# Half of the grouped attention's weights turned by VectorE blocks and DMA instead of TensorE, values two groups behind; the first sequence of the first attention turned by TensorE

## The chip, the cores and the metric

One core of a Trainium2 chip runs one kernel, from the inputs in DRAM to the output in DRAM. The metric is the device time in microseconds of that one launch. All data are fp32. PE is TensorE, DVE VectorE, ACT ScalarE, POOL GpSimd; SP issues the DMAs.

## What is computed

Eight sequences of 256 tokens with 512 features go through four layers in turn. Layers 0 to 2 begin with attention, and that is what the change touches. Layer 0: RMS norm with a conditioned scale, 8 query heads of 64 on one key and value head, rotary positions, softmax, values, output projection, residual; then a gated MLP. Layer 1: 16 heads of 32 with normed queries and keys, then a GELU MLP. Layer 2 has a grouped attention, and no MLP:

```
h = layernorm(x) * (1 + scale) + shift
q = rope(h @ Wq.T)                     # 16 heads of 32
c = h @ Wkd.T                          # 128 latent features
k, v = rope(c @ Wku.T), c @ Wvu.T      # 4 key and value heads of 32
s = q @ k.T / sqrt(32)                 # a key head for 4 query heads
s = where(mask, -inf, s)               # later blocks of 128 and all beyond a window of 64,
                                       # but for every 64th key, are hidden
x = x + (softmax(s) @ v) @ Wo.T
```

Layer 3 applies eight small experts to slices of the features, then a conditioned norm and a projection.

## The kernel before

The x of all sequences stays in SBUF as 16 tiles of 128 tokens. The layers follow each other: attention 0 (some 0 to 290 us of the profile), MLP 0 (to 905), attention 1 (to 1250), MLP 1 (to 1660), grouped attention (1672 to 1941), layer 3.

All three attentions are written by one function, `attend`. Its loop runs over 8 sequences and the groups of a sequence, four heads each: 2 groups in attention 0, 4 in the others. For a group it issues:

- the scores (`scored`, L692): for each head and block of 128 queries a matmul into one of four PSUM banks "A"; a bank is free again when the softmax of the head that was in it is done with it. In the grouped attention the first 128 queries see 128 keys and the others 256, so a head has 384 columns.
- the softmax (`softmax`): in the grouped attention DVE adds the mask and takes the row maximum in one custom instruction, with a second one that reads the accumulator into `low` (L730; in attention 0 it is a plain maximum, L714). ACT takes the exponential with the row sum (L734). A reciprocal of the sums (L745), a small DVE transpose (L749) and two DMAs over DRAM (L752, L757) spread the inverse sums.
- the turning of the weights, since the values product needs keys on partitions. There are two ways. By PE: 128x128 transposes against the identity (`turned`, L769) into a bank "C", and a copy back to SBUF (L478 on DVE for even places, L481 on ACT for odd ones). In blocks, for heads 0 and 1 of a group: the scores are taken with the keys in block order, the exponentials go to one tile for both heads, DVE turns its 32x32 blocks (L739), four DMAs put the tile to a DRAM tile `flip` (`put`, L546), and one gets it back (L743); the block of the right partitions then lies in place. `in_blocks` tells how many heads of a group go in blocks: two in attention 0 and 1 for sequences 0 to 6, none for sequence 7, none in the grouped attention.
- the values product one group behind (`weighted`, L794), and the multiplication with the inverse sums into the context (`divided`, L811).

Between these steps a queue of other work is fed in by portions (`some`, `quantum`): the projection of the next sequence (`project0`, `project2`: L628 from hT and wqkv; DVE's rope at L646 and L647; POOL's sums at L1650 and L1655; the copies at L1642 and L1654; the turned queries and keys at L1236 and L1242 with copies at L478 to L482) and the output projection of the last one (L628 from wo, addition to x at L1293). The portions come from costs written by hand in the call (`work`).

The input hT of a projection is prepared for a later sequence: norms (L448 to L468), DVE block transpose (L532), put to DRAM (L546), `fetch` back (eight DMAs, L564), and `modulate`, which scales it by DVE (L488) and ACT (L489) in turn. In attention 0 the norms are turned by PE (L498).

Attention 0 starts with the loads; DVE works out the angles of the rotary positions (`angles`: L1160 to L1192), ACT their sines (L1193 to L1196); PE works out conditions from weights that come from DRAM (L315, L333).

Within a program each engine takes its instructions in a fixed order, and SP its DMAs. That order comes from a scheduler of the framework, which starts from the order of the program's text; it isn't written out by hand. So a change in the text can move instructions that it does not name.

Of the kernel before, what the change touches and what calls it, by code (L numbers as in the profile page):

```python
# [34 lines left out]
P = 128  # L35
B, S, D = 8, 256, 512
NT = B * S // P
TB = S // P
# [59 lines left out]
def constants():  # L98

    f32 = np.float32  # L100
    freqs = (f32(1.0) / f32(10000.0) ** (np.arange(0, 32, 2, dtype=f32) / f32(32))).astype(f32)
    ang = np.arange(S, dtype=f32)[:, None] * freqs[None, :]
    cos = np.cos(ang.astype(np.float64)).astype(f32)
    sin = np.sin(ang.astype(np.float64)).astype(f32)
    rope = np.stack([np.concatenate([cos, cos], 1), np.concatenate([-sin, sin], 1)], 1)
    rope = rope.reshape(TB, P, 2, 32).transpose(1, 0, 2, 3)
    i, k = np.arange(S)[:, None], np.arange(S)[None, :]
    hidden = ((np.abs(k - i) > 64) & (k % 64 != 0)) | (k // P > i // P)
    mask = np.where(hidden, f32(MASKED), f32(0.0))
    mask = np.concatenate([mask[:P, :P], mask[P:, :]], 1)  # L110
    return {
        "inv_freq": np.array([INV_FREQ], f32),
        "rope2": np.ascontiguousarray(rope),
        "mask2": np.ascontiguousarray(mask),
    }


# [61 lines left out]
class Program:  # L179
# [357 lines left out]

    def in_blocks(self, name, b):

        return 2 if name != "attention2" and b < B - 1 else 0  # L540

    def put(self, kept, tile):

# [106 lines left out]


    def attend(self, name, n_groups, hd, project, value, finish, work, key_tiles=(2, 2), biased=None,
               extra=None, then=None, spare=None, inverse=None, after=None):

# [41 lines left out]
        def softmax(s, b):  # L698
            n_blocks = self.in_blocks(name, b)
            tot = self.t([P, 4, TB], "tot", 3)  # L700
            lows = self.t([P, 4, TB], "low", 3)

            blocks = self.t([P, 8 * P], "p")[:, : 2 * total]
            if n_blocks:
                put = blocks.rearrange("p (c h x) -> p h c x", c=4, h=2)
                ps = []
            else:
                ps = [blocks[:, j * total : (j + 1) * total] for j in range(2)]
            plain = self.t([P, 2, 512], "p")
            ps += [plain[:, j, :total] for j in range(2)]  # L710
            for j in range(4):
                low = lows[:, j, :]
                if biased is None:
                    nc.vector.tensor_reduce(  # L714
                        low, s[j].rearrange("p (q k) -> p q k", q=TB), AX.X, ALU.max, negate=True
                    )
                for q in range(TB):
                    cols = slice(at[q], at[q] + wide[q])
                    src, sign, out = s[j][:, cols], 1.0, None
                    if j >= n_blocks:  # L720
                        out = ps[j - n_blocks][:, cols]
                    else:
                        out = put[:, j, :, at[q] // 4 : (at[q] + wide[q]) // 4]
                        src = src.rearrange("p (c x) -> p c x", c=4)
                    if biased is not None:
                        by = biased[j < n_blocks][:, cols]
                        if j < n_blocks:
                            by = by.rearrange("p (c x) -> p c x", c=4)

                        nc.vector.tensor_tensor_reduce(  # L730
                            out, src, by, -1.0, BIG, ALU.add, ALU.min, low[:, q : q + 1]
                        )
                        src, sign = out, -1.0
                    nc.scalar.activation(  # L734
                        out, src, AF.Exp, bias=low[:, q : q + 1], scale=sign,
                        accum_out=tot[:, j, q : q + 1],
                    )
                if j == 3 and n_blocks:
                    nc.vector.transpose(blocks, blocks)  # L739
                    kept = self.flips[self.n_flip % 4][:, : 2 * total]  # L740
                    self.n_flip += 1
                    self.put(kept, blocks)
                    nc.sync.dma_start(blocks, kept)  # L743
            inv = self.inv[self.n_spread % 2]
            nc.vector.reciprocal(  # L745
                inv[:, 0 : 4 * TB].rearrange("p (j q) -> p j q", q=TB), tot
            )
            inv_t = self.t([P, 32], "invT", 2)
            nc.vector.transpose(inv_t, inv)  # L749

            kept = self.spread[self.n_spread % 4]
            nc.sync.dma_start(kept.rearrange("c (b r) -> b c r", b=4), inv_t)  # L752
            rows = kept.rearrange("(j q) t -> j (q t)", q=TB)
            by = []
            for c in range(nch):
                t = inverse[(self.n_spread * nch + c) % 4]
                nc.sync.dma_start(  # L757
                    t, rows[c * per : (c + 1) * per, :].unsqueeze(1).to_broadcast([per, hd, S])
                )
                by.append(t)  # L760
            self.n_spread += 1
            return (blocks, ps), by
# [43 lines left out]
        def divided(b, o, by):  # L806
            for c in range(nch):
                chunks = ctx.setdefault(b, [])
                out = spare()[len(chunks)] if b == late else self.t([P, S], "ctxT")
                in_ = o[:, c * S : (c + 1) * S]  # L810
                nc.vector.tensor_tensor(out, in_, by[c], ALU.mult)  # L811
                chunks.append(out)

        def outcome(b):
            chunks = ctx.pop(b)
            return finish(b, lambda k, t: chunks[k][:, t * P : (t + 1) * P])

        last, steps, done = None, [], []
        for i in range(B * n_groups + 1):
            ahead = None  # L820
            if i < B * n_groups:
# [18 lines left out]
                    turned(j + len(weights) % 4 // 2, p)  # L840
            if ahead is not None:
                ahead = (b, g, softmax(ahead[2], b))
                if g == 0 and ahead_of:
                    for c in (1, 2) if b == 0 else (b + 2,):
                        if c < B:
                            steps.append(self.prepare(name, c, quick=c == 1))
                        elif c == B and after is not None:
                            steps.append(self.prepare(after, 0))
                elif g == 0 and b == B - 1:
                    steps.append(self.prepare(after, 0))  # L850

                for step in steps:
                    for _ in step:
                        if b > 0 and ahead_of:
                            break
                    else:
                        done.append(step)
                steps[:] = [step for step in steps if step not in done]
# [17 lines left out]
                self.end = end  # L876
            else:
                self.some(quantum)
                b, g, (pT, by) = last
                weights = pT[1]  # L880
                for j, p in enumerate(weights[len(weights) // 2 :]):
                    turned(j + len(weights) % 4 // 2, p)
                self.some(quantum)
                divided(b, weighted(b, g, pT), by)
                if g == n_groups - 1:
                    if b != late:
                        self.queue.insert(0, outcome(b))
                    got.pop(b)
                self.some(quantum)
            if ahead is not None and ahead[1] == n_groups - 1:  # L890
                self.modulate()
# [726 lines left out]
    def load_layer2(self):  # L1618
        nc, d = self.nc, self.d
        w = self.t([P, KC, 1536], "wqkv", pool=self.wqkvp)  # L1620
        self.load(w[:, :, 0:512], "wq2T")
        self.load(w[:, :, 512:640], "wkdT")
        nc.sync.dma_start(w[:, 0, 640:896], d["wkvuT"])
        self.w2 = w
        self.w2o = self.t([P, KC, D], "wo", pool=self.wop)
        self.load(self.w2o, "wo2T")
        rope = self.bank("row")[:, 0 : TB * 64].rearrange("p (t c s e) -> p t c s e", t=TB, c=2, s=2)
        nc.sync.dma_start(rope.rearrange("p t c s e -> p t c (s e)"), d["rope2"])
        self.rope2 = rope
        self.mask = self.bank("row")[:, :384]  # L1630
        nc.sync.dma_start(self.mask, d["mask2"])

    def project2(self, b, got):
        nc, w = self.nc, self.w2
# [38 lines left out]
    def layer2(self):  # L1673
# [2 lines left out]
        self.attend(  # L1676
            "attention2", 4, 32, self.project2, lambda v, g, j, k: v[:, k, j * 32 : (j + 1) * 32],
            lambda b, ctxT: self.added(b, ctxT, self.w2o), (10.4, 6.8), key_tiles=(1, 2),
            biased=(self.mask,), extra={7: (self.expert_inputs(0), 1.74)},
            spare=lambda: [spare[:, i, :] for i in range(4)],  # L1680
            inverse=[spare[:, i, :] for i in range(4, 8)],
        )


# [178 lines left out]
```

## Time and profile before

| | |
|---|---|
| three runs, median | 2103.41 us (2102.42 to 2107.41) |
| the profiled execution | 2102.78 us |
| its span | 2100.7 us |
| mean granted clock of TensorE | 0.989 |
| DMA: moved, share of 16 engines | 182.48 MB, 29.3% |
| ACT exponentials L734, 128x256 (and others) | x512, 240.0 us |
| PE transposes of weights L769 | x816, 122.3 us |
| DVE mask and maximum L730 | x400, 127.8 us |

How to read the profile. Times are in microseconds from the span's start, unless marked ns; L12 is line 12 of the kernel before. A group row gives line, engine, operation, out<-in by tile names, shapes and count, then busy time and the mean of one in ns, then the idle time of the engine just before these instructions and what ended most of it. A timeline row gives start, duration, engine, line, operation; a bracket at its end gives the idle time ahead of it and its releaser. The duration of one PE or ACT instruction overlaps with its neighbours, so prices are better read from start to start. PEld is the weight load, which lies beside PE's matmuls. PEclk is the clock that TensorE was granted, in tenths of full speed in the page, as a fraction in tables by stretch. A row of waits gives who waited for whom: total, times, longest.

### The profile page before, as it was taken

What the parts mean: (1) busy time and instruction counts of PE and PEld (TensorE: products, weight loads), DVE (VectorE), ACT (ScalarE), POOL (GpSimd) and SP (SyncE); (2) the same over time, 40 slices, a digit from 0 to 9 for tenths busy, and PEclk for the clock granted to TensorE, in tenths of its full rate; (3) what the DMA queues carried; (4) which work ended last, traced back from release to release, by engine and by line L of the source; (5) the groups of instructions that cost most, each with busy time, mean ns of one, the idle gap of its engine ahead of it and who ended that gap; (6) DMA issues with size and microseconds to landing.
All of it is one profiled execution on the core that took longest, in us unless ns stands there. A gap on an engine that the chain in (4) does not pass through costs nothing.

```text
span 2100.7 us, 36220 instructions
## 1 busy us (share of the span) xinstructions
PE 2034.6 (97%) x12946; PEld 1486.9 (71%) x12946; DVE 1348.9 (64%) x4432; ACT 743.7 (35%) x2330; POOL 302.7 (14%) x340
## 2 busy tenths in 40 slices
PE   7799999999999999999999999999999999999999
PEld 4455569999999999854544448999999755555444
DVE  6677766666676555756676675767666777676233
ACT  4233421111111111146566652222222265556543
POOL 1111200000000000054445621000000111010220
PEclk8999999999999999999999999999999999999999
DMA  9543451212130010335455542235211321210001
GB/s 317 161 139 94 115 202 39 72 42 64 62 108 26 16 32 16 97 95 140 130 145 142 150 132 87 86 92 155 63 46 36 89 44 38 58 38 21 9 36 40
DMA packets 202659, 182.48 MB, mean 87 GB/s; under 512 B 81200, under 2 KB 169200, under 8 KB 202480
## 3 DMA queue, kind: packets, MB, share of 16 engines
q1 hardware_dynamic: 202480, 180.17, 29.3%
q8 instruction: 103, 1.69, 0.3%
q14 instruction: 76, 0.62, 0.1%
HBM read 122.16 MB, written 57.97 MB: 86 GB/s over the span
## 4 chain that ended last, share of the span: by engine, by line
PE 82%; DVE 6%; ACT 6%; DMA 3%; POOL 2%; issue 1%; SPq 0%; ACTq 0%; DVEq 0%; POOLq 0%
PE C L1002 28%; PE C L628 21%; PE A L1051 18%; ACT p L734 4%; PE A L692 4%; PE C L794 3%; PE C L769 3%; PE A L1731 1%; PE C L1750 1%; ACT p L481 1%; DVE st L448 1%; DVE p L730 1%; DMA hT<-turn 1%; PE C L315 1%; DVE n L647 1%
## 5 line engine op out<-in xcount | busy, mean ns | idle before, releaser
L1002 PE MATMUL C<-hT,wbig 128*128 128x128 f32 x3072 | 416.4, 275 | 1.0 <-DVE p L1025 1.0
L1002 PEld LDWEIGHTS C<-hT,wbig 128*128 128x128 f32 x3072 | 388.7, 192 | 10.1 <-issue 3.5
L628 PE MATMUL C<-wqkv,hT 128*128 128x512 f32 (+1 forms) x768 | 314.7, 551 | 0.4 <-ACT v L1490 0.4
L734 ACT ACTIVATE p<-p,low 128x256 f32<-128x256 f32 (+1 forms) x512 | 240.0, 471 | 165.8 <-DVE low L730 154.5
L1051 PE MATMUL A<-wbig,p 128*128 128x256 f32 x1024 | 242.2, 379 | 0.0
L628 PEld LDWEIGHTS C<-wqkv,hT 128*128 128x128 f32 x768 | 131.7, 193 | 122.7 <-issue 108.7
L1051 PEld LDWEIGHTS A<-wbig,p 128*128 128x128 f32 x1024 | 189.7, 190 | 23.1
L1032 DVE TENSOR_TENSOR p<-p,C 128x256 f32<-128x256 f32 x192 | 79.0, 419 | 164.3 <-PE C L1002 162.3
L1022 ACT COPY p<-C 128x128 f32<-128x128 f32 x192 | 50.8, 265 | 367.5 <-PE C L1002 359.0
L628 PE MATMUL C<-wo,ctxT 128*128 128x512 f32 x336 | 159.8, 609 | 2.9 <-DVE ctxT L811 2.9
L1002 PE MATMUL C<-ctxT,wbig 128*128 128x128 f32 x1152 | 160.0, 275 | 0.0
L1002 PE MATMUL C<-qk,wbig 128*128 128x128 f32 x1152 | 159.8, 275 | 0.0
L456 POOL TENSOR_SCALAR r<-mv 128x2 f32<-128x2 f32 (+1 forms) x28 | 7.0, 252 | 967.7 <-DVE mv L449 967.7
L730 DVE CUSTOM_DVE_ANT_0 p<-A,row 128x256 f32<-128x256 f32 (+1 forms) x400 | 127.8, 377 | 26.6 <-PE A L692 24.9
L1002 PEld LDWEIGHTS C<-ctxT,wbig 128*128 128x128 f32 x1152 | 144.1, 192 | 0.0
L1002 PEld LDWEIGHTS C<-qk,wbig 128*128 128x128 f32 x1152 | 144.0, 192 | 0.0
L769 PEld LDWEIGHTS C<-ident,p 128*128 128x128 f32 x816 | 92.2, 142 | 64.3 <-issue 37.8
L769 PE MATMUL C<-ident,p 128*128 128x128 f32 x816 | 122.3, 282 | 4.8 <-DVE p L478 1.9
L1374 ACT ACTIVATE p<-C 128x128 f32<-128x128 f32 x64 | 17.7, 277 | 302.4 <-DVE p L1032 302.4
L1023 DVE TENSOR_TENSOR p<-p,C 128x128 f32<-128x128 f32 x192 | 54.7, 285 | 96.6 <-ACT p L1022 95.6
L628 PEld LDWEIGHTS C<-wo,ctxT 128*128 128x128 f32 x336 | 59.5, 191 | 67.7 <-issue 55.2
L734 ACT ACTIVATION_READ_ACCUMULATOR p<-p,low 128x1 f32 x512 | 96.2, 188 | 0.0
(227 smaller groups left out, 3224.6 us busy)
## 6 DMA issues: line engine op xcount, KB each, us to landing
flip<-p SPq DMA_DIRECT2D x168, 128.0 KB
p<-flip SPq DMA_DIRECT2D x42, 512.0 KB
turn<-hT SPq DMA_DIRECT2D x120, 128.0 KB
hT<-turn SPq DMA_DIRECT2D x16, 512.0 KB
kept<-hT SPq DMA_DIRECT2D x16, 512.0 KB
hT<-kept SPq DMA_DIRECT2D x16, 512.0 KB
wbig<-spread SPq DMA_DIRECT2D x64, 128.0 KB
hT<-turn SPq DMA_DIRECT2D x112, 64.0 KB
```

Source lines behind the costliest of these rows:

```text
L315: self.nc.tensor.matmul(m[32 * i : 32 * i + 32, :], cond[:, k, :], w[c // 512][:, k, c % 512 : c % 512 + width], start=(k == 0), stop=(k = ...
L628: self.nc.tensor.matmul(out, lhsT(k), rhs(k), start=(k == 0), stop=(k == n - 1))
L692: nc.tensor.matmul(s[j][:, at[q] : at[q] + wide[q]], lhsT(q), keys, start=True, stop=True,)
L730: nc.vector.tensor_tensor_reduce(out, src, by, -1.0, BIG, ALU.add, ALU.min, low[:, q : q + 1])
L734: nc.scalar.activation(out, src, AF.Exp, bias=low[:, q : q + 1], scale=sign, accum_out=tot[:, j, q : q + 1],)
L769: nc.tensor.transpose(m[:, n * P : (n + 1) * P], p[:, at[q] + k * P : at[q] + (k + 1) * P], self.ident,)
L794: mm = nc.tensor.matmul(o[i * hd : (i + 1) * hd, c * S + q0 * P : (c + 1) * S], value(got[b][1], g, j, k), weights(j, mine), start=(k == 0 ...
L1002: nc.tensor.matmul(m[:, c : c + P], w[:, k * P : (k + 1) * P], b[:, k], start=(first and k == 0), stop=(k == steps - 1), skip_group_check= ...
L1022: nc.scalar.copy(g[:, 0, :], m[:, 0:P])
L1023: nc.vector.tensor_tensor(g[:, 0, :], g[:, 0, :], m[:, P : 2 * P], ALU.add)
L1032: nc.vector.tensor_tensor(g[:, 1:3, :], g[:, 0, :].unsqueeze(1).to_broadcast([P, 2, P]), m[:, 2 * P : 4 * P].rearrange("p (i t) -> p i t", ...
L1051: nc.tensor.matmul(acc[at][:, half * S : (half + 1) * S], left, right, start=(p == 0 and half == 0), stop=(p == 3), skip_group_check=True,)
```

## The change

In the grouped attention heads 0 and 1 of each group of sequences 0 to 6 are turned in blocks; sequence 7 stays with PE. The copies of the two heads that PE still turns both go to ACT. Each group's weights lie in one of four "rooms" (tiles of 128x2048), its contexts in halves of one tile for two sequences; the mask is held a second time in block order, loaded by one more DMA. The values product of these groups stands two groups behind (`lag`, `due`), not one. In attention 0 sequence 0 is turned by PE, not in blocks.

By count, before and after: L769 in the program 816 and 664; DVE copies of 128x384 in the grouped attention 56 fewer; DVE block transposes of 128x768 28 more, of 128x1024 two fewer; puts and gets of `flip` 140 more in the grouped attention and ten fewer in attention 0; in attention 0 four more DVE copies of 128x512. The order of the instructions differs on all engines in these two attentions, and is the same in the MLPs and in attention 1.

```diff
@@ in_blocks
-        return 2 if name != "attention2" and b < B - 1 else 0
+        first = {"attention0": 1, "attention1": 0, "attention2": 0}[name]
+        return 2 if first <= b < B - 1 else 0
@@ softmax
-            blocks = self.t([P, 8 * P], "p")[:, : 2 * total]
+            if rooms is None:
+                blocks, plain = self.t([P, 8 * P], "p"), self.t([P, 2, 512], "p")
+            else:
+                room = rooms[self.n_spread % 4]
+                blocks, plain = room[:, : 8 * P], room[:, 8 * P :]
+                plain = plain.rearrange("p (j x) -> p j x", j=2)
+            blocks = blocks[:, : 2 * total]
...
-            plain = self.t([P, 2, 512], "p")
@@ divided
-                out = spare()[len(chunks)] if b == late else self.t([P, S], "ctxT")
+                if b == late:
+                    out = spare()[len(chunks)]
+                elif contexts is not None:
+                    out = contexts[:, b % 2 * 4 + len(chunks), :]
+                else:
+                    out = self.t([P, S], "ctxT")
@@ the loop over groups
+                lag = 2 if rooms is not None and self.in_blocks(name, b) else 1
+                due.append((i + lag, *ahead))
...
-                divided(b, weighted(b, g, pT), by)
-                if g == n_groups - 1:
-                    if b != late:
-                        self.queue.insert(0, outcome(b))
-                    got.pop(b)
+                while due and due[0][0] <= i:
+                    _, b, g, (pT, by) = due.pop(0)
+                    divided(b, weighted(b, g, pT), by)
+                    if g == n_groups - 1:
+                        if b != late:
+                            self.queue.insert(0, outcome(b))
+                        got.pop(b)
@@ load_layer2
-        self.mask = self.bank("row")[:, :384]
+        self.mask = both[:, TB * 64 :]
         nc.sync.dma_start(self.mask, d["mask2"])
+        self.mask_blocks = self.bank("row")[:, :384]
+        nc.sync.dma_start(self.mask_blocks, d["mask2_blocks"])
@@ layer2
-            biased=(self.mask,), extra={7: (self.expert_inputs(0), 1.74)},
+            biased=(self.mask, self.mask_blocks), extra={7: (self.expert_inputs(0), 1.74)},
...
+            rooms=[self.t([P, 4 * 512], "wbig") for _ in range(4)],
+            contexts=self.t([P, 8, S], "wbig"),
```

## The prediction

> **What bounds the kernel now.** First the page: busy times, granted clock and the chain that ended last.
>
> ```profile
> PE 2034.6 (97%) x12946; PEld 1486.9 (71%) x12946; DVE 1348.9 (64%) x4432; ACT 743.7 (35%) x2330; POOL 302.7 (14%) x340
> ...
> PEclk8999999999999999999999999999999999999999
> ...
> PE 82%; DVE 6%; ACT 6%; DMA 3%; POOL 2%; issue 1%; SPq 0%; ACTq 0%; DVEq 0%; POOLq 0%
> ```
>
> TensorE is the bound: only 66 us of the 2100.7 us span are not PE work. An edit gains what it takes off PE and loses every PE idle that it opens. Next the groups of the grouped attention (1672 to 1941 us), shapes kept apart:
>
> ```profile
> L769 PE MATMUL C<-ident,p 128*128 128x128 f32 x372 | 54.7, 280 | 3.4 <-DVE p L478 1.9 <-ACT qT L482 1.5
> ...
> L478 DVE COPY p<-C 128x384 f32<-128x384 f32 x62 | 33.9, 546 | 0.4
> ```
>
> These are the weights' transposes and their copies by VectorE. The mean of 280 ns overlaps with its neighbours, so the price is read from PE's timeline, at the start of a sequence:
>
> ```profile
> 1848.33 0.94 PE L692 MATMUL A<-v,qT 32*128 32x128 f32 x16
> 1849.19 0.98 PE L769 MATMUL C<-ident,p 128*128 128x128 f32 x7
> 1850.02 1.89 PE L628 MATMUL C<-hT,wqkv 128*128 128x256 f32 x8
> 1851.74 1.88 PE L628 MATMUL C<-wqkv,hT 128*128 128x512 f32 x4
> 1853.56 1.37 PE L794 MATMUL C<-p,kT 128*32 128x256 f32 x16
> ```
>
> From start to start seven transposes take 0.83 us, 119 ns each, a group's scores (L692) 0.86 us. After the first scores of a sequence stands the projection of the next (L628 from hT), without any idle. The table by stretches says how full each engine is, and when the clock was halved (columns: length, PE, PEld, DVE, ACT, POOL busy, granted clock, DMA share, GB/s):
>
> ```profile
> 289.60:293.00 3.40, 1.62 (x3) 0.59 (x4) 1.00 (x5) 0.00 (x0) 0.00 (x0) 1.00 0.14 48
> 293.00:296.40 3.40, 3.40 (x5) 1.34 (x4) 2.43 (x6) 0.00 (x0) 0.00 (x0) 0.50 0.83 237
> ...
> 914.30:917.70 3.40, 2.21 (x13) 1.38 (x13) 3.40 (x14) 0.94 (x4) 0.00 (x0) 1.00 0.98 358
> 917.70:928.00 10.30, 10.30 (x32) 6.44 (x31) 8.07 (x34) 7.37 (x28) 0.00 (x0) 0.50 0.29 82
> ...
> 1740.30:1743.70 3.40, 2.09 (x22) 1.30 (x19) 3.09 (x13) 1.78 (x6) 1.68 (x2) 1.00 0.04 7
> 1849.00:1858.00 9.00, 9.00 (x66) 5.03 (x59) 5.50 (x25) 4.62 (x19) 0.00 (x0) 1.00 0.23 56
> 1815.00:1849.40 34.40, 32.85 (x232) 17.97 (x231) 24.72 (x112) 19.52 (x77) 3.38 (x4) 1.00 0.23 49
> ```
>
> One sequence of the grouped attention is the last row: PE 32.9 of 34.4 us, DVE 24.7, ACT 19.5. Last, PE's waits, and ACT's timeline in the longest:
>
> ```profile
> PE C L1242 <- ACT v L481: 10.3, 1, 10.3
> ...
> PE C L794 <- DMA p<-flip: 1.5, 1, 1.5
> ```
>
> ```profile
> 65.27 0.52 ACT L1193 ACTIVATE row<-row 128x384 f32<-128x384 f32 x1 [16.30 <-DVE row L1192]
> ...
> 67.17 0.24 ACT L481 COPY v<-C 128x128 f32<-128x128 f32 x1
> ```
>
> In the first attention PE stands for 10.3 us since a copy of v waits on ACT behind a sine that waits for DVE's angles.
>
> **Transposes and copies.** In 28 groups (seven sequences by four) 6 of 12 transposes go: 168 x 0.119 = 20.0 us off PE; by the tightest and loosest pace that I find in the trace (0.109 and 0.135) 18.3 to 22.7. The two copies per group go from DVE: 56 starts at 0.47 (L478 at 1851.51, the next at 1851.98), 26.3 us; one DVE transpose of 128x768 comes. The trace has that of 1024 columns in the second attention:
>
> ```profile
> L739 DVE STREAM_TRANSPOSE p<-p 128x1024 f32<-128x1024 f32 x28 | 34.8, 1244 | 5.8 <-ACT p L734 5.8
> ```
>
> Three quarters are 0.93 us, 28 times 26 us. DVE's sum stays the same, with 9.7 us free in a sequence. L730 in block form costs what the plain form costs (418 and 419 ns per 256 columns in the second attention): nothing. Here a rule speaks against the change: the Trainium skill, "VectorE: DVE Perf Modes", Rules for kernel authors, gives a full 128x128 transpose to TensorE. It looks at the operation alone (390 ns there, against 311 by DVE in 32x32 blocks, both for bf16). By it the six transposes stay where they are and the gain is zero; by the rows PE has 119 ns each and is the bound, DVE 155 (0.93 / 6) with time to spare, so the 20.0 us stand.
>
> **The DMAs.** Per group SP issues four puts and one get more, 140 in all, 0.8 MB moved in a group's 8.6 us, about 90 GB/s beside 49; the DMA share is 0.23. Two groups (17 us) lie between turn and use; in the second attention one group was enough but for a single wait of 1.5 us. So the weights arrive: nothing (0 to 2 us). But the puts wait on SP for DVE's transpose, and the fetch of the next hT now stands behind them, in order.
>
> **What moves: the starts of sequences.** In the compiled order of the changed program the modulation of hT (L488, L489) is no longer ahead of a sequence's first softmax, as in before (L488 at 1846.79), but behind two of them at four of the seven starts (sequences 3 to 6), and PE has the scores of groups 1 and 2 directly behind group 0, ahead of the projection. The scores need banks that DVE's softmax frees, the modulation needs ACT. I walk one start with the rows of before; zero is the end of the first scores. ACT takes 0.89 us a head (1849.68 to 1850.57): group 0's exponentials run from 0.3 to 3.8, a copy (0.36) to 4.2, group 1's to 7.7. DVE takes 0.555 a head (four in 1849.28 to 1851.51): group 0 to 2.2, block transpose to 3.1, group 1 to 5.8, its transpose after two heads' exponentials, 6.1 to 6.9, first L488 to 7.3; the first L489 on ACT after 7.7, to 8.1. PE can run the projection without a break from about 8.2. Its own work until then: rest of the scores 0.4, three transposes 0.36, two groups' scores 1.7, a quarter of the projection 0.65: 3.1. Idle: 5.1 us (4.5 to 5.7 with the signals between engines), where before had none (9.00 of 9.00). Four starts: +20.4 us. Everything behind is late with it: the values product stands behind the projection, and group 2's softmax waits for that product's room. The start of sequence 2 has half of it, +3 (2.5 to 4); at the first sequence the later values leave PE less to do beside the softmaxes, +1.5 (0 to 3).
>
> **The clock.** In such a start PE is busy 3.1 of 8.2 us, 38%. Rows: a stretch of 3.4 us with PE busy 1.62 was followed by 3.4 us at half clock, one with 2.21 by 10.3 us, one with 2.09 by none. At half clock that costs 1.7 and 5.1 us. The rule, the Trainium skill, "TensorE: Matmul & The Clock Gate", HAM oscillation, asks only for no idle gap above some 3.4 us; bursts of scores break ours, so by the rule nothing is lost. The rows have the say, as 1.62 of 3.40 has no such gap either: I take 2.6 us at each of four starts, +10.4, ends 0 and 20.
>
> **First attention.** Sequence 0 gives its two groups back to PE: 16 transposes more, +1.9 us on PE; two DVE transposes and ten DMAs less, off the path. In the new order ACT's copy of v stands ahead of the sines and DVE's copies ahead of most angles, so the 10.3 us wait goes. The added transposes come just there, and next to be late are the transposed norms and group 0's values; walking them through, PE reaches the second half of that product 7 us earlier than at 84.7. I take -6.5 with the transposes in it (-4 to -9); after that PE is full (48.2 of 48.8 us), so it lasts.
>
> **Sum.** -20.0 + 20.4 + 3 + 1.5 + 10.4 - 6.5 = +8.8 us. The profiled execution took 2102.78 us (span 2100.7 and 2.1 around it), 0.6 below the median of 2103.41; on the median this gives 2112.
>
> **Rivals.** *Idle without the half clock* (0.24): the same sum less 10.4, -1.6: 2102, no change. For it: 2.09 of 3.40 without consequence; against it: 38% is lower than that.
> *The faster side, starts that cost little* (0.26): hT modulated and the scores freed with some 1.5 us lost per start, so -20.0 + 6 + 3 - 6.5 = -17.5: 2086. It decides from a start's idle of about 3.5 us downward (without half clock, -8). For it: DVE and ACT are not full over a sequence, and PE, not they, sets the sum; against it: the order is fixed, and two groups' exponentials are 7 us by themselves.
> *The first attention gains nothing* (0.06), since another wait takes over: +15.3, 2119.
> *The weights late from DRAM* (0.04): each of 28 products 1 us late, +28 on the likeliest without clock: 2130. The one 1.5 us wait in the second attention speaks against it.
> The likeliest (0.40) is slower: 2112.
>
> **Chances.** A measurement of this kernel tells 0.3%, 6.3 us, from no change. Faster by more: the 0.26 and a little of the idle case, 0.28. Within: the rest of that case and the low end of the likeliest, 0.25. Slower: 0.47. The range reaches into the faster case, and up to 20 us of half clock: 2084 to 2127.
>
> **What would show it.** L769 some 664 times, not 816, and 56 fewer L478 copies: the removal. PE idle of 4 to 6 us within the first 9 us of sequences 3 to 6, named as L692 waiting for DVE's low (L730) or L628 for hT (L488, L489): the starts; a sequence then takes some 37 us, not 34.4. Granted clock 0.5 behind them: the clock. PE's wait for v gone at 57 us and the first MLP entered 6 us earlier: the first attention. Wrong I would be if those starts show PE full, or if the values wait for the flips' DMA.

## The result, and the profile after

Fourteen runs of each kernel: 2108.61 us after (2103.80 to 2110.78), 2104.85 before (2102.09 to 2111.13). The ratio is 1.0015, with an interval of 1.0007 to 1.0022: slower by 1.5 to 4.6 us, less than the 0.3% that the prediction counts as a change. The forecast of 2112 had the sign right and was too high by some 5 us in the difference. The profiled execution after took 2104.45 us, 1.7 more than that of before. From here on, lines of code are numbered as in the kernel whose trace is shown. In the changed kernel L696 are the scores, L778 PE's transposes, L739 mask and maximum, L743 exponentials, L748 the block transpose, L803 the values product, L630 projections, L489 and L490 the modulation of hT, L566 its fetch. The experiments' kernels have the same lines a few numbers further on; tile names and operations tell them.

The page of the changed kernel, the same three lines as before:

```profile
PE 2033.2 (97%) x12794; PEld 1488.9 (71%) x12794; DVE 1351.7 (64%) x4406; ACT 746.9 (36%) x2330; POOL 304.0 (14%) x340
...
PEclk9999999999999999999999999999999999989999
...
PE 79%; DVE 7%; ACT 7%; DMA 3%; POOL 2%; issue 2%; SPq 1%; ACTq 0%; DVEq 0%; POOLq 0%
```

PE has 152 matmuls less and is busy for only 1.4 us less; PE's share of the chain fell from 82% to 79%, while those of DVE and ACT rose from 6% to 7% each. Where the time went is seen by stages, from the first matmul of a stage in the two traces:

| stage | before | after | difference |
|---|---|---|---|
| first attention, to the first MLP's first matmul | 283.9 | 279.7 | -4.2 |
| first MLP to the start of the grouped attention | 1389.6 | 1390.7 | +1.2 |
| grouped attention, to layer 3 | 267.6 | 273.0 | +5.4 |
| layer 3, to PE's last | 155.9 | 155.2 | -0.7 |

And the grouped attention by sequences, from first scores to next first scores (the last: to layer 3):

| sequence | 0 | 1 | 2 | 3 | 4 | 5 | 6 | 7 |
|---|---|---|---|---|---|---|---|---|
| before | 37.4 | 34.1 | 34.4 | 34.4 | 34.4 | 34.4 | 28.9 | 29.4 |
| after | 37.0 | 29.8 | 33.2 | 35.7 | 37.8 | 37.7 | 30.6 | 31.2 |

Sequence 1 shows what was gained, 4.3 us; sequences 3 to 6 lose more than that again. The timeline that follows shows PE in the changed kernel at the start of sequence 4. It is to be set beside that of before at 1848.33, in the prediction, which starts a sequence of the same kind:

```profile
1806.10 1.03 PE L696 MATMUL A<-kT,qT 32*128 32x128 f32 x16
1807.06 0.55 PE L778 MATMUL C<-ident,wbig 128*128 128x128 f32 x3
1807.94 2.49 PE L696 MATMUL A<-kT,qT 32*128 32x128 f32 x16 [0.33 <-DVE low L739]
1811.04 0.89 PE L696 MATMUL A<-kT,qT 32*128 32x128 f32 x4 [0.60 <-DVE low L739]
1812.08 2.66 PE L696 MATMUL A<-kT,qT 32*128 32x128 f32 x12 [0.16 <-DVE low L739]
1815.69 1.22 PE L630 MATMUL C<-hT,wqkv 128*128 128x256 f32 x2 [0.94 <-DVE hT L489]
```

Three groups' scores stand in a row, each head waiting for a bank, and the projection begins 8.63 us after the transposes that follow the first scores (L778 at 1807.06, L630 at 1815.69); in before it was 0.83 (1849.19 to 1850.02). DVE and ACT in the same stretch:

```profile
1813.26 0.98 DVE L748 STREAM_TRANSPOSE wbig<-wbig 128x768 f32<-128x768 f32 x1 [0.21 <-ACT wbig L743]
1815.01 0.20 DVE L754 RECIPROCAL inv<-tot 128x8 f32<-128x8 f32 x1 [0.77 <-ACT wbig L743]
1815.22 0.73 DVE L489 TENSOR_SCALAR hT<-hT,mod 128x256 f32<-128x256 f32 x2
```

The modulation comes after the second group's block transpose and after a reciprocal that waits for ACT's last exponential. The stretches of that sequence, with the columns as before:

```profile
1806.10:1843.93 37.83, 34.97 (x208) 19.18 (x207) 25.71 (x108) 19.96 (x78) 3.41 (x4) 0.91 0.49 128
1807.06:1815.69 8.63, 6.50 (x40) 4.24 (x36) 7.31 (x39) 8.21 (x35) 0.00 (x0) 0.81 0.63 146
1812.40:1819.20 6.80, 5.86 (x18) 3.81 (x17) 2.56 (x10) 3.56 (x14) 0.00 (x0) 0.50 0.59 167
```

ACT is nearly full in the 8.63 us (8.21): it sets their length. From 1812.40, still within this stretch, the clock is halved for 6.8 us; the same stands at sequences 3, 5 and 6, and 3.4 us at sequence 2. Note that PE counts as busy for 6.50 of 8.63 us there. At the pace of before its work there, three transposes and two groups' scores, is some 2 us: a lone head's scores are shown as long. Groups and waits of the changed kernel:

```profile
L778 PE MATMUL C<-ident,wbig 128*128 128x128 f32 x204 | 33.7, 281 | 0.8 <-DVE mv L450 0.3 <-DVE n L649 0.2 <-ACT qT L483 0.2
...
L748 DVE STREAM_TRANSPOSE wbig<-wbig 128x768 f32<-128x768 f32 x28 | 27.3, 976 | 3.5 <-ACT wbig L743 3.5
```

```profile
PE A L696 <- DVE low L739: 11.1, 16, 3.7
...
PE C L334 <- DVE n L330: 3.5, 1, 3.5
```

The transposes fell from 372 records to 204; the block transposes take 0.98 us each. Of the 11.1 us for low, 4.5 lie at the starts of sequences 2 to 6. The wait of 10.3 us for v in the first attention is gone; the nearest long one is 3.5 us for the conditions' rows (L330).

### The profile page after: what moved, and what is told of

Read it like the earlier page. It is cut to its first block, busy times and chain, and to the rows that moved or that the text cites. A ratio compares the mean times of both kernels' runs of the same rounds, so it can differ in the third digit from the quotient of the medians.

```text
span 2102.3 us, 36198 instructions
## 1 busy us (share of the span) xinstructions
PE 2033.2 (97%) x12794; PEld 1488.9 (71%) x12794; DVE 1351.7 (64%) x4406; ACT 746.9 (36%) x2330; POOL 304.0 (14%) x340
## 4 chain that ended last, share of the span: by engine, by line
PE 79%; DVE 7%; ACT 7%; DMA 3%; POOL 2%; issue 2%; SPq 1%; ACTq 0%; DVEq 0%; POOLq 0%
PE C L1019 28%; PE C L630 20%; PE A L1068 18%; PE A L696 3%; ACT p L743 3%; PE C L803 3%; PE C L778 2%; ACT wbig L743 2%; PE A L1753 1%; PE C L1772 1%; DMA hT<-turn 1%; DVE wbig L739 1%; DVE st L449 1%; DVE n L649 1%; ACT p L482 1%
## 5 line engine op out<-in xcount | busy, mean ns | idle before, releaser
L630 PE MATMUL C<-wqkv,hT 128*128 128x512 f32 (+1 forms) x768 | 317.1, 553 | 1.3 <-ACT hT L483 0.9
L630 PEld LDWEIGHTS C<-wqkv,hT 128*128 128x128 f32 x768 | 133.4, 194 | 121.4 <-issue 106.1
L743 ACT ACTIVATE p<-p,low 128x256 f32<-128x256 f32 x256 | 126.8, 497 | 70.7 <-DVE low L739 62.3
L743 ACT ACTIVATE wbig<-wbig,low 128x128 f32<-128x128 f32 (+1 forms) x256 | 113.2, 444 | 75.9 <-DVE low L739 73.6
L696 PE MATMUL A<-kT,qT 32*128 32x256 f32 (+2 forms) x896 | 97.4, 399 | 9.9 <-DVE low L739 9.1
L630 PE MATMUL C<-wo,ctxT 128*128 128x512 f32 x224 | 103.6, 601 | 3.1 <-DVE ctxT L825 3.1
L696 PEld LDWEIGHTS A<-kT,qT 32*128 32x128 f32 (+1 forms) x896 | 62.1, 190 | 50.9 <-issue 32.1
L739 DVE CUSTOM_DVE_ANT_0 wbig<-A,row 128x128 f32<-128x128 f32 (+1 forms) x256 | 75.1, 349 | 34.9 <-PE C L803 23.6
L1495 POOL TENSOR_TENSOR ss<-ss,neg_half 128x16 f32<-128x16 f32 x32 | 93.6, 2925 | 2.7
```

What stands on the lines that cost most here:

```text
L630: self.nc.tensor.matmul(out, lhsT(k), rhs(k), start=(k == 0), stop=(k == n - 1))
L696: nc.tensor.matmul(s[j][:, at[q] : at[q] + wide[q]], lhsT(q), keys, start=True, stop=True,)
L739: nc.vector.tensor_tensor_reduce(out, src, by, -1.0, BIG, ALU.add, ALU.min, low[:, q : q + 1])
L743: nc.scalar.activation(out, src, AF.Exp, bias=low[:, q : q + 1], scale=sign, accum_out=tot[:, j, q : q + 1],)
L1495: nc.gpsimd.tensor_tensor(r, r, self.neg_half[:, 0:16], ALU.pow)
```

## The experiments

Two explanations stand against each other. *The starts*: the transposes earn what was reckoned, and the loss sits at the starts of sequences alone, where hT is late in SP's queue, its modulation slips behind two softmaxes, the scheduler puts scores ahead of the projection, and the clock falls. *The flips*: the DVE transposes, the DMAs and the longer way of the values cost it in every group. Times below are differences worked out from the ratio to the kernel before on the same chip, times 2104; the brackets are 95% intervals of the ratio.

**The two parts apart.** One is before with the first attention's part alone, the other the changed kernel with `"attention0": 0`.

```diff
-        return 2 if name != "attention2" and b < B - 1 else 0
+        return 2 if name != "attention2" and (name == "attention0") <= b < B - 1 else 0
```

> The kernel before with only the first attention's part: its sequence 0 turned by TensorE. Both theories read the two traces alike here: the first MLP is entered 4.2 us earlier, 3.1 us of it are left at the grouped attention, so 2.5 to 4 us faster than before. If a gain of the first attention were only an accident of one execution, the ratio would hold 1.0.

> The changed kernel with the first attention as before: only the grouped attention's part. If the two parts add, it is slower than before by 5 to 8 us (the stage took 5.4 us longer, and the gain of the first attention is missing). If they interact over the phase of the clock, by less than 3 or more than 10 us.

Measured: 0.9988 (0.9981 to 0.9994), 2.5 us faster; 1.0026 (1.0016 to 1.0037), 5.5 us slower. The sum, +3, is the change's +3.2: the parts add.

**The fetches by another queue.**

```diff
-                    self.nc.sync.dma_start(to[:, k, t], parts[:, k, t])
+                    self.nc.gpsimd.dma_start(to[:, k, t], parts[:, k, t])
```

> The changed kernel with the eight fetches of the next hT issued by POOL instead of SP, so that they don't stand behind the puts and gets of the flips. In the compiled order the modulation is back in the first softmax of a sequence and the projection directly behind its first scores. Theory of the starts: 20 us of transposes gained and hardly any idle or half clock at the starts, so 18 to 24 us faster than the changed kernel, some 2086 us. Rival (the flips' DMAs, the block transposes and the later values cost it in every group): within 5 us of the changed kernel, with PE waiting for values or softmax in all groups.

Measured: 1.0029 (1.0020 to 1.0038), 6.1 us slower than before: a miss. POOL got to the fetches late too, as its timeline shows ahead of the sequence that starts at 1819.62:

```profile
1818.42 0.46 POOL L1675 TENSOR_TENSOR kr<-kr,n 128x128 f32<-128x128 f32 x1 [11.65 <-PE C L1259]
1818.94 5.95 POOL L566 DMA_DIRECT2D hT<-turn  x8
```

PE then waited for hT at the starts (up to 4.2 us for L490). The fetch had been moved, but not the four puts ahead of it: SP issued the last of them only at 1814.23, behind puts of the flips. What made the whole slower lies elsewhere: the second attention's fetches were moved as well, and ahead of its first scores PE waited 6.8 us for sums of POOL (L1499), so that it began 9.5 us later than in the changed kernel. The grouped attention itself took 270.4 us, 2.6 less than in the changed kernel. So the run doesn't support the flips (no wait for them came up), and it mends the starts only in small part.

**The scores kept in order, fetches on SP.**

```diff
-                        nc.tensor.matmul(
+                        mm = nc.tensor.matmul(
...
+                        if rooms is not None:
+                            self.tc.keep_in_program_order(mm)
```

> The changed kernel with the grouped attention's scores kept in the order of the program, fetches on SP as they are. PE then has the projection behind the first scores of a sequence again, while the modulation of hT still comes behind one softmax of the sequence. Theory of the starts: if the scores put ahead are what costs, 15 to 20 us faster than the changed kernel; if it is the late hT itself, PE waits for hT (L488, L489) some 3 us at each start and it is 0 to 8 us faster. Rival (flips in every group): within 5 us.

Measured: 0.9965 (0.9952 to 0.9978), 7.4 us faster than before, some 10.5 faster than the change: between the two readings. What is left is seen at the start of its sequence 3, on PE, DVE and SP's queue:

```profile
1773.13 2.90 PE L630 MATMUL C<-hT,wqkv 128*128 128x256 f32 x6 [4.45 <-DVE hT L489]
```

```profile
1774.17 0.41 DVE L489 TENSOR_SCALAR hT<-hT,mod 128x256 f32<-128x256 f32 x1 [1.15 <-DMA hT<-turn]
```

```profile
1764.26 0.94 SPq L548 DMA_DIRECT2D turn<-hT  x2
1765.25 1.32 SPq L548 DMA_DIRECT2D flip<-wbig  x2
1768.52 5.26 SPq L566 DMA_DIRECT2D hT<-turn  x8
```

The projection waits 4.45 us for hT, and hT for its own DMA. SP needs 5.3 us for the eight issues alone, and they begin 1.35 us after the sequence (1767.17). In before they ran from 1826.47 to 1833.6 and were done 14.7 us ahead of the sequence at 1848.33:

```profile
1826.47 1.23 SPq L564 DMA_DIRECT2D hT<-turn  x2
...
1829.08 2.69 SPq L564 DMA_DIRECT2D hT<-turn  x4
...
1832.40 1.21 SPq L564 DMA_DIRECT2D hT<-turn  x2
```

SP issues twenty DMAs in a sequence of before and forty in the changed kernel; from its timeline they take 11.9 of 34.4 us and 21.9 of 37.8. So SP isn't full. It is the order in its queue that delays hT. For the changed kernel's start at 1806.10 DVE's transpose of hT, SP's puts and its fetch are these, then two rows of before:

```profile
1757.91 1.25 DVE L533 STREAM_TRANSPOSE hT<-hT 128x1024 f32<-128x1024 f32 x1
```

```profile
1793.91 0.72 SPq L548 DMA_DIRECT2D turn<-hT  x1
...
1797.57 1.51 SPq L548 DMA_DIRECT2D turn<-hT  x3
1802.95 0.79 SPq L548 DMA_DIRECT2D flip<-wbig  x2
1803.91 5.87 SPq L566 DMA_DIRECT2D hT<-turn  x8
```

```profile
1818.12 1.25 DVE L532 STREAM_TRANSPOSE hT<-hT 128x1024 f32<-128x1024 f32 x1
```

```profile
1819.39 0.31 SPq L546 DMA_DIRECT2D turn<-hT  x1
```

In before the first put follows the transpose at once, 28.9 us ahead of the sequence that uses it. In the changed kernel DVE's transpose stands earlier than before (48 us ahead of its use for 30), but the first put comes 36 us after it (transposes and puts matched by their order) and 12.2 us ahead of the sequence. SP issued twenty puts of flips in between, and the fetch begins 2.2 us ahead instead of 21.9. That the scheduler puts the scores ahead of the projection because it expects hT late is inferred; the next runs test the lateness itself.

**hT one group earlier, with the order, and alone.** In the first group of a sequence two steps of the preparation are taken instead of one. Only the lines that do this are shown.

```diff
...
                         if b > 0 and ahead_of:
+                            if rooms is not None and g < 2 and id(step) not in twice:
+                                twice.append(id(step))
+                                continue
                             break
```

> The kernel with scores in program order, and in the grouped attention two steps of hT's preparation in the first group of a sequence, so that its puts and fetches reach SP's queue one group earlier. If what is left of the starts' cost is hT landing late behind SP's issues (PE waited 4.5 us for L489 at the worst start of that kernel, and sequences took 31 to 36.6 us), every sequence takes 31 to 32 us and it is 6 to 12 us faster than that kernel, some 2088 us. If the flips cost it elsewhere (DVE's block transposes, the bound moved to ACT or DVE), it stays within 3 us of it.

> The changed kernel with hT prepared one group earlier and nothing else: the scores of groups 1 and 2 still stand partly ahead of the projection in the compiled order (two groups' scores around it). If the lateness of hT in SP's queue is the whole cause, as fast as with scores in order too, some 2089 us. If the order of the scores counts by itself, between that and the changed kernel: some 2095 to 2103 us, with idle on DVE's low at the starts.

Measured: 0.9920 (0.9905 to 0.9935), 16.8 us faster than before; alone 0.9934 (0.9916 to 0.9953), 13.9 faster. The intervals overlap: once hT is early, keeping the order adds nothing that these runs can tell. A rest remains in both. With the order, sequences 4 and 5 took 34 us with 1.9 us of idle and 3.4 us of half clock, sequences 1 to 3 30.4 to 31. Without it they took 33.8 and 35.4, with a group's scores still ahead of the projection and 6.8 us of half clock.

**A control.** Both edits were made on the kernel before.

> Control: the kernel before, without blocks in the grouped attention, with scores in program order and hT prepared early. If the gain of these two edits is only that they remove what the change brought about at the starts, this is the kernel before within 3 us. If they are a gain of their own, it is faster than before by up to 10 us, and that is to be taken off from what the blocks earn.

Measured: 1.0012 (1.0003 to 1.0022), 2.5 us slower. The edits earn nothing by themselves; they only take back what the change brought about. Here too SP's puts follow DVE's transpose within some 1.5 us, as in before.

**How far behind the values have to be.** The kernel with the order and this edit:

```diff
-                lag = 2 if rooms is not None and self.in_blocks(name, b) else 1
+                lag = 1
```

> The kernel with scores in program order, values of the groups turned in blocks one group behind instead of two. If a group (7.5 us) is enough for block transpose, four puts and a get with SP's issues of 0.45 to 0.65 us, the same time within 3 us. If it isn't, PE waits for the flips' DMA in most of the 28 groups, 1 to 3 us each: 20 to 60 us slower.

Measured: 1.0028 (1.0018 to 1.0038), 13 us slower than the same kernel with two groups (0.9965). PE's waits name it:

```profile
PE C L805 <- DMA wbig<-flip: 25.4, 9, 4.0
```

One group is not enough here; two are: with them PE waits for these DMAs 0.8 us in all at most (order and early hT), and not at all in the changed kernel.

**What the clock counts.** Two fillers into the bank ahead of the scores of groups 1 and 2 of sequences 2 to 6: transposes of the identity, or the head's first scores once more.

```diff
+                        if q == 0 and rooms is not None and g in (1, 2) and 2 <= b <= 6:
+                            for _ in range(2):
+                                nc.tensor.transpose(s[j][:, 0:P], self.ident, self.ident)
```

> The changed kernel with two transposes of the identity (128 rows of the array active) into the bank ahead of each head's scores in groups 1 and 2 of sequences 2 to 6: 80 more in ten groups, 9.5 us of PE work, most of it in idle time of the starts. In the compiled order sequences 4 to 6 start as in the changed kernel. Theory of rows (the clock gate counts how much of the array works, and scores use 32 of 128 rows): no half clock at the starts of sequences 4 to 6, and these sequences 1 to 2 us shorter in spite of the filler. Theory of busy time: no difference from the filler of 32 rows.

```diff
+                        if q == 0 and rooms is not None and g in (1, 2) and 2 <= b <= 6:
+                            nc.tensor.matmul(
+                                s[j][:, at[q] : at[q] + wide[q]], lhsT(q), keys, start=True, stop=True)
```

> The same with the filler that has only 32 rows active: the first 128 columns of each head's scores in groups 1 and 2 of sequences 2 to 6 are computed once more in the same place, 40 matmuls or 80 blocks of the moving side like the other filler. Sequences 5 and 6 start as in the changed kernel. Theory of rows: half clock at the starts of sequences 4 to 6 as in the changed kernel (6.8 us each). Theory of busy time: it is gone as with 128 rows, since PE is busy for longer.

Measured: 1.0069 (1.0053 to 1.0084) and 1.0011 (1.0002 to 1.0020). The start of sequence 4, first with the 128-row filler, then with the other:

```profile
1813.40:1816.80 3.40, 3.07 (x20) 1.94 (x17) 3.21 (x17) 2.92 (x13) 0.00 (x0) 1.00 0.49 76
1816.80:1827.00 10.20, 9.73 (x33) 5.41 (x33) 4.18 (x22) 5.68 (x23) 0.00 (x0) 0.50 0.66 158
```

```profile
1810.10:1813.50 3.40, 2.32 (x23) 1.84 (x21) 2.85 (x18) 3.40 (x17) 0.00 (x0) 1.00 0.50 78
1813.50:1820.30 6.80, 6.76 (x29) 4.83 (x30) 3.34 (x17) 4.22 (x18) 0.00 (x0) 0.50 0.71 160
```

At sequences 4 to 6 half clock came with both, even after a stretch in which PE shows 3.07 of 3.40 us busy. Busy time as the profile shows it isn't what decides, and the forecast for the 128-row filler failed. But that doesn't rule out the rows: with this filler the clock stayed full at the starts of sequences 2 and 3, where the changed kernel had it halved for 3.4 and 6.8 us (with the other filler, at 2 alone). The order of the matmuls at these two starts isn't quite that of the changed kernel.

A sum over the fourteen traces speaks for the rows. The times between changes of the clock are multiples of 3.41 us (3.4, 6.8, 10.2 and so on). For each stretch of this grid, taken 0.1 us earlier, add up the columns of the matmuls that start in it, each times its rows / 128: a score of 32 rows and 128 columns gives 32, a transpose 128. From 75 us on there are 8090 such stretches at full clock. All 77 with a sum below 1536 were followed by half clock; of the 8013 others 15 were. Without the 0.1 us a line at 1536 misplaces 20. No line drawn through busy time misplaces fewer than 45, none through columns without rows fewer than 54, none through a sum without transposes fewer than 79. Some of the sums:

| stretch that starts at | busy, as shown | sum | next |
|---|---|---|---|
| 914.3, before | 2.21 | 768 | half |
| 1740.3, before | 2.09 | 2560 | full |
| 1813.4, filler of 128 rows | 3.07 | 1472 | half |
| 1779.2, filler of 128 rows | 3.29 | 1536 | full |
| 1810.1, filler of 32 rows | 2.32 | 928 | half |

In the changed kernel the five stretches ahead of half clock have 768 to 1472. So the 128-row filler was too little at sequences 4 to 6. This is a reading after the fact, with a line fitted to these traces. The 15 cases stay unexplained, and no run has tested it: what is counted stays open, with the rows as the best candidate.

**The best version.** It has the order, early hT, and the grouped attention's fetches issued by ACT; only the last edit is shown.

```diff
...
-                    self.nc.sync.dma_start(to[:, k, t], parts[:, k, t])
+                    (self.nc.scalar if name == "attention2" else self.nc.sync).dma_start(to[:, k, t], parts[:, k, t])
```

> The kernel with scores in order and hT prepared early, and the grouped attention's eight fetches of hT issued by ACT instead of SP. In the compiled order both pairs of modulations come ahead of a sequence's first softmax from the fourth sequence on. If what is left (2 us of idle and 3.4 us of half clock at the worst starts) is hT late behind SP's issues, the starts show no idle and no half clock, sequences take some 31 us, 3 to 10 us faster than that kernel. If ACT pays for the issues (8 times 0.65 us in a sequence, ahead of exponentials), it is no faster or slower by some us.

Beside it stands a floor, from the kernel with order and early hT. It leaves out the flips (block transpose, puts and get), so that its values product reads weights that are not turned; only its time is of use:

```diff
-                if j == 3 and n_blocks:
+                if j == 3 and n_blocks and rooms is None:
```

> Scores in order and hT early, but heads 0 and 1 of the grouped attention are not turned at all: DVE's block transpose, the four puts and the get of each group are left out, so the values product reads weights that are not turned. It is the floor for any way to turn them beside PE. By the sum 18 to 23 us of transposes less than before and 2 to 4 of the first attention: 2079 to 2085 us, without idle and half clock at the starts. If it is no faster than the kernel with the flips, SP's issues and DVE's transposes cost nothing there any more.

Measured: 0.9886 (0.9868 to 0.9905), 2081.02 us beside 2104.01, 24 us faster than before; the floor 0.9865 (0.9848 to 0.9882), 28 us. By the stage, the grouped attention took 247.4 us and 241.4, for 267.6 in before. Sequences 3 and 4 take 30.3 to 30.4 us in both. PE's timeline of the best version at a start, and one sequence of it; then one of the floor:

```profile
1803.03 0.55 PE L780 MATMUL C<-ident,wbig 128*128 128x128 f32 x3
1803.41 1.89 PE L630 MATMUL C<-hT,wqkv 128*128 128x256 f32 x8
1805.14 1.88 PE L630 MATMUL C<-wqkv,hT 128*128 128x512 f32 x4
```

```profile
1801.61:1831.95 30.34, 28.62 (x207) 15.18 (x206) 25.45 (x108) 19.41 (x79) 3.70 (x4) 1.00 0.59 158
```

```profile
1796.91:1827.25 30.34, 28.55 (x207) 15.19 (x206) 21.79 (x104) 19.46 (x78) 3.69 (x4) 1.00 0.25 55
```

No idle after the first scores, full clock. The flips' 3.7 us on DVE and their DMAs (0.59 beside 0.25) cost nothing in the steady sequences: there the second explanation is out. Outside them some cost may be left, as the stage is 6.0 us longer than the floor's: sequences 1, 2 and 6 take 2.3, 2.8 and 1.5 us more, and sequence 2 has half clock at its start. The floor also shows what holds up the puts: without the flips SP issues the first put of hT 1.3 us after DVE's transpose (1753.96 and 1755.23).

## Why the prediction was right, and where its sizes were off

The direction was right, and so was the mechanism at the starts; that the number came so near is in part luck, since errors of several us in its terms made up for each other.

*Transposes and copies.* The mechanism held, the size was low. The prediction had 24 x 0.119 = 2.9 us for a sequence. In the steady sequences PE's transposes fell from 48 to 24 and from 5.9 to 2.9 us, as reckoned; but the values product takes 3.2 us, not 4.3, though it has as many matmuls. In all a steady sequence is 4.1 us shorter (34.43 to 30.34). Taken for all seven that is 28.7, not 20.0; it is an estimate, since sequences 0 and 6 differ, and in the stage the floor is 26.2 us below before and the best version 20.2. Why the product is shorter was not tried. By the rule of the Trainium skill, "VectorE: DVE Perf Modes", Rules for kernel authors, which gives a full transpose to TensorE, nothing was to be gained. It doesn't hold for this case, where TensorE is the bound: the best version keeps half of the turning off TensorE in seven sequences and is 24 us faster than before, some 3 of them from the first attention.

*The DMAs.* "So the weights arrive: nothing" was right for two groups. The row it leaned on, that one group was enough in the second attention, didn't carry over (25.4 us of waits with one group). That the fetch of hT now stands behind the flips' puts was named. Making hT early, and nothing else, takes back 17 us of the loss, the best version 27. What wasn't followed up is that hT's own puts stand there too, 36 us behind DVE's transpose.

*The starts.* The walk gave 8.2 us to a projection without a break; it began at 8.63, at half the clock. The losses by sequence, if each of 0 to 6 gained 4.1 us: 3.7, -0.2, 2.9, 5.3, 7.5, 7.4, 5.8 for sequences 0 to 6, and 1.7 for sequence 7. For sequence 2 the prediction had 3, for 3 to 6 7.7 each with the clock (30.8 in all, measured 26.0), for sequence 0 1.5; sequence 7 it didn't have.

*The clock.* It was halved at all four starts for 6.8 us, and for 3.4 at sequence 2. The rule of the Trainium skill, "TensorE: Matmul & The Clock Gate", HAM oscillation, on idle gaps would have given none: the longest gap at the start shown is 0.94 us. The rows decided rightly, but by luck: their 1.62, 2.21 and 2.09 are busy time as shown, while 3.1 of 8.2 is work at full pace. As shown PE was busy for 6.50 of 8.63 us, more than in any of these rows. What the half clock cost can be estimated from the trace. At sequence 4 its first 3.3 us fall where ACT sets the pace; the projection ran at half clock for the other 3.5 us (1815.69 to 1819.20), a loss of some 1.8. With 2.7, 3.2 and 3.1 us at sequences 3, 5 and 6 that is some 6 us in all for the 10.4 of the prediction, and some 20 of the 26.0 are waiting, for 20.4. No run parted the two.

*First attention.* -6.5 was too much: 4.2 us at the first MLP, 2.5 by the run of this part alone. The 10.3 us wait did go; what was next to be late was not the norms but the conditions' rows:

```profile
56.64 5.37 PE L316 MATMUL C<-wbig,scondT 128*32 128x256 f32 x64
...
66.53 1.11 PE L334 MATMUL C<-ident,n 128*128 128x128 f32 x4 [3.46 <-DVE n L330]
```

*The sum.* By terms: -28.7 for -20.0; +34.1 at the starts for +35.3; so +5.4 in the stage for +15.3; and -2.5 to -3.1 for -6.5. Two terms were mis-sized, by 8.7 and by 3.4 to 4.0 us, and partly made up for each other; the first of them, what is saved when the transposes go (the values product behind them included), is the step that took the result from slower by more than 0.3% to within it, the case that had a chance of 0.25.

## What to carry to other kernels

Before work is moved from a full engine to DMAs, look at what already stands in the queue that will issue them, and behind what each of its transfers will come to stand; count the issues as an engine's time as well (here twenty more in a sequence, 10 us of SP). Here the input of the next projection came late behind the new puts, and that cost more than the replaced transposes earned. When a well-founded saving doesn't show, look for the transfer that became late, start it earlier or from a queue that is free at that time, and try again before the idea is given up: here +3 us became -24.

## What the runs showed of the hardware

- An SP issue took 0.34 us (the get of a flip) to 0.63 us (a fetch of hT) in the median, single ones up to 2.0; the eight fetches of hT (pieces of 32 elements) 5.3 to 5.9 us on SP and 6.0 on POOL.
- The granted clock fell to 0.5 behind stretches in which PE shows 2.3 to 3.1 of 3.4 us busy, when much of this was scores that came head by head; in before it stayed full behind 2.09 us of other work. Busy time isn't what decides. Columns weighted by rows, transposes counted in full, put 8075 of 8090 stretches on the right side of one line (1536 in 3.41 us).
- The block transpose of 128x768 took 0.98 us; three quarters of the 1.24 us of 128x1024 are 0.93.
